# First layer of a four-layer image network: rescaled rows on GpSimd in slot 8, two of a band's four layer norm operations on VectorE

## Chip, cores and metric

The kernel runs on one core of a Trainium2 chip. The metric is the device time of one execution in microseconds (us); the lower the better. All data are float32.

## What is computed

The reference takes an image batch `x` of shape (4, 64, 64, 128) and adds four residual layers to it in turn: `x = x + layer(group_norm(x))`. Only the first layer matters here. It is a selective scan over the 4096 pixels of each image in four directions:

```python
xz = x @ in_proj_w.T                       # x is the group-normed image
xh, z = jnp.split(xz, 2, axis=-1)          # 256 channels each
z  = silu(z)
xc = silu(depthwise_conv3x3(xh) + conv_b)
xs = [xc by rows, xc by columns, both reversed]        # K = 4 directions
...                                        # delta, B, C: small projections of xs
h  = exp(delta * A) * h + (delta * u) * B  # step by step over 4096 pixels, 16 states
y  = sum(h * C) + D * xs                   # the four directions are added
y  = (y - mean) / sqrt(var + eps) * out_norm_w + out_norm_b    # layer norm of a pixel
y  = y * z
out = y @ out_proj_w.T
```

The other three layers (Fourier mixing, a Fourier neural operator with attention, neighbourhood attention) follow after it and are the same code before and after the change.

## The kernel before

**Units and slots.** The first layer walks through 128 units: 4 images, 4 directions, 8 chunks of 512 pixels. A unit has 16 slots, one for each of the 16 states, so there are 2048 slots. The numbers of slots below run from 0 to 15 in a unit. In every slot the code issues the following, in this order:

- GpSimd: `dB = du * B` (line 699, 128x1024). There are three `dB` buffers, so GpSimd can be up to three slots ahead of the scans.
- VectorE: what was put off to this slot with `later("dve", ...)`, and then the steps that `TABLE` gives it.
- ScalarE and VectorE, twice (once for each half of the channels): `dA = exp(delta * A)` into one of three PSUM banks (line 704) and the scan `h` (`tensor_tensor_scan`, line 705), which reads `dA` and `dB`.
- TensorE: eight transposes of an older slot's `h` into the single PSUM tile `pt` (line 549), and eight products `yT` with C (line 584). ScalarE copies `pt` to `hT` (line 559).
- What was put off to `act2`, which is the last place of the slot on ScalarE.
- TensorE: steps of the next unit's projections, such as `dp` (line 475), and in slots 10 and 12, after the `dB` of that slot, GpSimd's `du = delta * u` (line 487). `du` waits for VectorE's `delta` of slots 9 and 11 (line 484).

**Order.** The order on each engine is the order in which the code issues, written out by hand (`tc.manual_schedule`). `later(place, f, ..., slots=n)` puts an operation off by `n` slots.

**Side work.** Two generators are threaded through the slots, one piece at a time. A piece runs in a slot that the sets of `SIDE` allow for its kind, and when its share of the unit's slots is due.

- `before(b + 1)` prepares the next image while image b is scanned: statistics, then for each of eight chunks `c` a DMA `load` of ten padded rows (`xn`), the operation `scaled`, which applies the group norm to `xn` in place (line 326), two products for the gate z (kind `z`, slots 13 and 1), and for each half `s` a 3x3 convolution as nine TensorE pieces `t` = 0 to 8 (kind `c`, starting in slot 11 and then one in every slot up to slot 3 of the next unit; line 159). The rows of chunk `c + 1` are loaded at piece (s, t) = (0, 0) of chunk `c`, and scaled after piece (1, 5). One chunk takes three units.
- `after(b)` finishes image b while image b + 1 is scanned, in eight bands of 512 pixels. For images 0 and 1 (`b + 2 < NB`), piece `t` computes `nb = 1/sqrt(var + eps)` on ScalarE (line 388), puts off the small product `mb = -mean * nb` (a 128x4 operation on VectorE) by two slots, and puts off the four normalisations `y[:, q, :] = y * nb + mb` (128x256) on ScalarE by two, three, four and five slots. Two pieces `m` transpose the band to `pg` and ScalarE writes it to `yg`; GpSimd multiplies by z in slot 7 (line 414); the output projection follows in slot 8 (line 424).

For image 2 the normalisations are done by the existing helper `normed` on VectorE, with the factor in PSUM; image 3 has no following image. The helper, which the change also uses:

```python
nb = spare("nb")[:, 0:4]                      # images 2 and 3: PSUM
nb = small.tile([P, 4], F32, name="nb")       # images 0 and 1: SBUF
```

In the profile, operations that are issued by `flush` have the line of `later`'s list (L645) and are told apart by the names of their tiles: `mb`, `yf` (the band), `yg`, `e` (the steps of silu).

Of the kernel before, what the change touches and what calls it, by code (L numbers as in the profile page):

```python
# [12 lines left out]
AF = mybir.ActivationFunctionType  # L13
ALU = mybir.AluOpType
# [10 lines left out]
NCH = NT // CH  # L25
# [57 lines left out]
def layer0(sh, A, x_in, x_out, scr, ahead):  # L83
# [6 lines left out]
    tc, nc = sh.tc, sh.nc  # L90
    with ExitStack() as ctx:
# [60 lines left out]
        def conv(xn, s, bank, out):  # L152

            for t in range(9):
                yield "c"
                if t == 0:
                    pm = bank("cv")
                dy, dx = divmod(t, 3)
                nc.tensor.matmul(  # L159
                    pm,  # L160
                    lhsT=taps[:, s, t, :],
                    rhs=xn[:, dy : dy + 8, dx : dx + 64],
                    start=(t == 0),
                    stop=(t == 8),
                )
            out.append(pm)
# [6 lines left out]
        def gates(b, c, v, bank, later, es=(None, None)):  # L173
            for s in range(2):
                yield "z"
                zp = bank("zp")
                nc.tensor.matmul(zp, lhsT=w_in[:, 2 + s, :], rhs=v, start=True, stop=True)
                silu(zp, 0.0, 0.0, scr(f"z{b % 3}")[s, :, c * CH : (c + 1) * CH], later, (("act0", 2), ("act0", 3), 4), es[s])
# [126 lines left out]
        def before(b, bank, later):  # L305

            st = small.tile([P, NCH, 6], F32, name="gn_st")
            for c in range(NCH):  # L310
                yield "l"
                t = tmp.tile([P, CH], F32, name="xs", tag="t2", bufs=4)
                nc.sync.dma_start(t.rearrange("p (h w) -> p h w", w=64), A["x_t"][b, :, 8 * c + 1 : 8 * c + 9, 1:65])
                yield "s"
                later("dve", nc.vector.bn_stats, st[:, c, :], t)
            yield "m"
            s_, o_ = sh.group_scale(st, psm, small, "m", exp_rstd)

            def load(c):
                xn = tmp.tile([P, 10, 66], F32, name="xn", bufs=3)  # L320
                nc.sync.dma_start(xn, A["x_t"][b, :, 8 * c : 8 * c + 10, :])
                return xn

            def scaled(xn, c, r0, r1):
                inner = xn[:, max(r0, int(c == 0)) : min(r1, 10 - int(c == NCH - 1)), 1:65]
                nc.scalar.activation(inner, inner, AF.Identity, scale=s_, bias=o_)

            yield "l"
            ahead = load(0)
            yield "x"  # L330
            later("act2", scaled, ahead, 0, 0, 10)
            for c in range(NCH):
                xn = ahead
                yield from gates(b, c, xn[:, 1:9, 1:65], bank, later)
                for s in range(2):
                    for t, piece in enumerate(conv(xn, s, bank, out := [])):
                        yield piece
                        if c < NCH - 1 and (s, t) == (0, 0):
                            ahead = load(c + 1)
                        if c < NCH - 1 and s == 1 and t == 5:  # L340
                            later("act2", scaled, ahead, c + 1, 0, 10)
                    grown(b, c, s, out[0], later)

        def silu(v, bias, minus, dst, later, wait, e=None):
# [22 lines left out]
        def after(b, st, later, bands):  # L367

            for c in bands:
                yield "l"  # L370
                rows = slice(c * CH, (c + 1) * CH)
                if kept:
                    y = kept.pop()
                else:
                    y = tmp.tile([P, 4, 2 * P], F32, name="yf", tag="t4", bufs=4)
                    nc.sync.dma_start(y, tiles(scr(f"y2{b % 2}")[rows, :]))
                z = tmp.tile([P, 2, CH], F32, name="zf", tag="t4", bufs=4)
                nc.sync.dma_start(z, scr(f"z{b % 3}")[:, :, rows].rearrange("s p t -> p s t"))
                mv = small.tile([P, 4, 2], F32, name="ln_mv")
                for q in range(4):  # L380
                    nc.vector.bn_aggr(mv[:, q, :], st[:, 4 * c + q])

                rs = small.tile([P, 4], F32, name="ln_r")
                later("act1", nc.scalar.activation, rs, mv[:, :, 1], AF.Ln, bias=sh.eps5)
                if b + 2 < NB:
                    yield "t"
                    nb = small.tile([P, 4], F32, name="nb")
                    nc.scalar.activation(nb, rs, AF.Exp, scale=-0.5)
                    mb = small.tile([P, 4], F32, name="mb")
                    later("dve", nc.vector.scalar_tensor_tensor, mb, mv[:, :, 0], -1.0, nb, ALU.mult, ALU.mult, slots=2)  # L390
                    for q in range(4):
                        norm = dict(scale=nb[:, q : q + 1], bias=mb[:, q : q + 1])
                        later("act2", nc.scalar.activation, y[:, q, :], y[:, q, :], AF.Identity, slots=2 + q, **norm)
                else:
                    yield "n"

                    nb = spare("nb")[:, 0:4]
                    nc.scalar.activation(nb, rs, AF.Exp, scale=-0.5)
                    for q in range(4):
                        later("dve", normed, y[:, q, :], mv[:, q, 0:1], nb[:, q : q + 1])  # L400
                yg = tmp.tile([P, 2, CH], F32, name="yg", bufs=2)
                for s in range(2):
                    yield "m"
                    pt = spare("pg")
                    for q in range(4):
                        nc.tensor.transpose(pt[:, q * P : (q + 1) * P], y[:, q, s * P : (s + 1) * P], sh.ident)
                    norm = dict(scale=on_w[:, s : s + 1], bias=on_b[:, s : s + 1])
                    later("act0", nc.scalar.activation, yg[:, s, :], pt, AF.Identity, **norm)
                yield "f"
                xr = tmp.tile([P, 4, DM], F32, name="xr", tag="t2", bufs=4)  # L410
                nc.sync.dma_start(xr, tiles(x_in(b)[rows, :]))
                if b < NB - 1 or c > 2:
                    yield "g"
                nc.gpsimd.tensor_tensor(yg, yg, z, ALU.mult)
                if b + 2 < NB:
                    yield "o"
                    op = psy.tile([P, 2, 2 * P], F32, name=f"yT{int(not rev)}").rearrange("p r d -> p (r d)")
                else:
                    yield "m"
                    op = spare("op")  # L420
                op = op.rearrange("p (q d) -> p q d", q=4)
                for q in range(4):
                    for s in range(2):
                        nc.tensor.matmul(
                            op[:, q, :], lhsT=yg[:, s, q * P : (q + 1) * P], rhs=w_out[:, s, :], start=(s == 0), stop=(s == 1)
                        )
                later("dve", residual, b, rows, xr, op, slots=2)
# [134 lines left out]
        def products(G, q, hT):  # L562
# [68 lines left out]
            c={11},  # L631
            g={7},
            s={11, 12, 13, 14, 15, 0, 1, 2, 3},
            t={11, 12, 15, 0},
            o={8},
            f=(),
            l=(),
# [3 lines left out]
        slot = 0  # L641

        def later(place, f, *a, slots=1, **kw):

            todo.setdefault((slot + slots, place), []).append(lambda: f(*a, **kw))  # L645
# [10 lines left out]
        with tc.manual_schedule(engines=order):  # L656
# [4 lines left out]
            for i, (b, k, c) in enumerate(units):  # L661
# [25 lines left out]
                for n in range(NS):  # L687
                    slot = NS * i + n
                    g, q = divmod(n, 4)
# [39 lines left out]
                    if n == 10:  # L729
                        y = unit["y"] = tmp.tile([P, 4, 2 * P], F32, name="y", tag="t4", bufs=4)  # L730
# [15 lines left out]
                        d.step()  # L746
                    for d in sides:
                        if d.need == "t" and n in SIDE["t"] and d.due(slot) and (inside or not any(o.taps for o in sides)):
                            d.free_at = slot + 6
                            d.step()  # L750
                        if d.need == "o" and n in SIDE["o"] and d.due(slot - 8):
                            d.step()
                        if d.need == "s" and n in SIDE["s"] and d.due(slot):
                            d.step()
                        if d.need in ("f", "l") and d.due(slot):
                            if d.need == "l":
                                d.free_at = slot + 3
                            d.step()
# [1455 lines left out]
```

## Time and profile before

| | us |
|---|---|
| median of 3 runs (lowest, highest) | 7645.87 (7638.12, 7647.14) |
| the profiled execution, its own time | 7645.85 |
| span of the profile, first to last instruction | 7644.1 |
| first layer in it, roughly | from 0 to 5600 |
| ScalarE `xn` (L326), 24 operations of 864 to 944 ns | 21.9 |
| ScalarE `yf` (L645), 64 operations, mean 604 ns | 38.7 |
| VectorE `mb` (L645), 16 operations, mean 1428 ns | 22.9 |

The page of the profile gives the busy time of each engine, the chain of work that ended last and the costliest groups of instructions. DVE is VectorE, ACT is ScalarE, POOL is GpSimd, PE is TensorE and PEld its weight loads. A group's line reads: line of the code, engine, operation, names of what is written and read, shapes, count, busy time in us and mean duration of one in ns, and after the bar the engine's idle time just before these instructions and what ended it. In a timeline, a line gives the start, the length, the engine and the instruction with the number of merged neighbours, and in brackets the idle time before it.

### The profile page before, as it was taken

What the parts mean: (1) busy time and instruction counts of PE and PEld (TensorE: products, weight loads), DVE (VectorE), ACT (ScalarE), POOL (GpSimd) and SP (SyncE); (2) the same over time, 40 slices, a digit from 0 to 9 for tenths busy, and PEclk for the clock granted to TensorE, in tenths of its full rate; (3) what the DMA queues carried; (4) which work ended last, traced back from release to release, by engine and by line L of the source; (5) the groups of instructions that cost most, each with busy time, mean ns of one, the idle gap of its engine ahead of it and who ended that gap; (6) DMA issues with size and microseconds to landing.
All of it is one profiled execution on the core that took longest, in us unless ns stands there. A gap on an engine that the chain in (4) does not pass through costs nothing.

```text
span 7644.1 us, 140402 instructions
## 1 busy us (share of the span) xinstructions
PE 6293.8 (82%) x52604; PEld 3973.6 (52%) x52604; DVE 6715.7 (88%) x7999; ACT 6135.0 (80%) x9771; POOL 5691.9 (74%) x2688
## 2 busy tenths in 40 slices
PE   7888888778898877888887777787789978686889
PEld 3554444444455544445554444454467756464556
DVE  7999999999999999999999999999956655656678
ACT  7999999999999999999999999999943323324667
POOL 4999999999999999999999999999920024123233
PEclk8999999999999999999999999999999988788999
DMA  6656566546667554565756445555533241331332
GB/s 181 171 177 176 182 175 180 171 154 178 198 180 195 184 179 160 167 196 178 183 191 180 165 169 180 179 185 174 190 92 73 59 120 46 83 99 46 102 95 82
DMA packets 1328925, 1160.66 MB, mean 152 GB/s; under 512 B 718709, under 2 KB 1119697, under 8 KB 1261298
## 3 DMA queue, kind: packets, MB, share of 16 engines
q1 hardware_dynamic: 1323970, 1149.24, 50.4%
q8 instruction: 414, 6.78, 0.4%
q10 hardware_dynamic: 4272, 2.43, 0.1%
q14 instruction: 269, 2.20, 0.1%
HBM read 958.19 MB, written 189.21 MB: 150 GB/s over the span
## 4 chain that ended last, share of the span: by engine, by line
ACT 36%; PE 31%; DVE 18%; issue 8%; POOL 3%; DMA 2%; SPq 1%; ACTq 0%; DVEq 0%; POOLq 0%
ACT hT L559 14%; ACT dA L704 14%; DVE h L705 12%; PE pt L549 5%; PE cv L159 3%; POOL dB L699 3%; PE yT L584 3%; PE pf L939 2%; PE po L952 1%; ACT e L645 1%; ACT delta L478 1%; PE yT L458 1%; PE pz L1183 1%; PE pt L1892 1%; ACT delta L481 1%
## 5 line engine op out<-in xcount | busy, mean ns | idle before, releaser
L705 DVE TENSOR_TENSOR_SCAN h<-dA,state,dB 128x512 f32<-128x512 f32 x4096 | 4927.0, 1266 | 120.7 <-ACT dA L704 72.4
L699 POOL TENSOR_TENSOR dB<-du,Bb 128x1024 f32<-128x1024 f32 x2048 | 4816.5, 2387 | 152.3 <-DVE h L705 118.2
L549 PE MATMUL pt<-ident,h 128*128 128x128 f32 x16384 | 2216.7, 278 | 859.2 <-ACT hT L559 833.8
L704 ACT ACTIVATE dA<-delta,A_neg 128x512 f32<-128x512 f32 x4096 | 2765.5, 696 | 102.7 <-DVE h L705 77.0
L549 PEld LDWEIGHTS pt<-ident,h 128*128 128x128 f32 x16384 | 1802.7, 141 | 1917.7 <-ACT hT L559 1700.5
L559 ACT COPY hT<-pt 128x1024 f32<-128x1024 f32 x2048 | 2080.7, 1016 | 125.5 <-PE pt L549 105.9
L584 PE MATMUL yT<-hT,W 128*32 128x256 f32 x16384 | 1378.6, 409 | 4.3 <-DVE xr L433 3.5
L584 PEld LDWEIGHTS yT<-hT,W 128*32 128x32 f32 x16384 | 456.2, 150 | 346.3 <-issue 324.3
L159 PE MATMUL cv<-xn,taps 128*128 128x512 f32 x936 | 527.1, 645 | 2.7 <-DVE delta L484 2.6
L1183 POOL TENSOR_TENSOR xg<-xg,so 128x1024 f32<-128x1024 f32 x16 | 39.3, 2469 | 622.8 <-PE pu L1183 622.2
L1930 POOL TENSOR_TENSOR S<-S,sm 128x784 f32<-128x784 f32 x128 | 191.1, 1493 | 416.3 <-DVE sm L1928 250.0
L487 POOL TENSOR_TENSOR du<-delta,u 128x512 f32<-128x512 f32 x256 | 327.8, 1281 | 163.6 <-DVE delta L484 162.2
L475 PE MATMUL dp<-xd,w_dt 65*128 65x512 f32 x512 | 288.7, 646 | 33.8 <-DVE delta L484 23.7
L458 PE MATMUL yT<-u,w_x 128*48 128x512 f32 x508 | 244.4, 604 | 21.3 <-DVE y L600 20.1
L1937 ACT ACTIVATE S<-S,mx 128x196 f32<-128x196 f32 x512 | 227.9, 448 | 33.2 <-DVE mx L1964 32.7
L159 PEld LDWEIGHTS cv<-xn,taps 128*128 128x128 f32 x936 | 139.2, 188 | 180.5 <-issue 160.4
L940 ACT ACTIVATE h<-pf,b 128x512 f32<-128x512 f32 x128 | 87.6, 687 | 118.8 <-PE pf L939 100.5
L484 DVE SCALAR_TENSOR_TENSOR delta<-delta,dp 128x512 f32<-128x512 f32 x256 | 169.7, 663 | 3.2 <-ACT delta L481 1.0
L1183 POOL TENSOR_TENSOR WX<-wr,Xs 128x544 f32<-128x544 f32 x40 | 59.3, 1483 | 149.1 <-issue 63.4
L1892 PE MATMUL pt<-ident,S 128*98 128x128 f32 x1024 | 165.6, 286 | 3.5 <-POOL S L1930 2.0
L481 ACT ACTIVATE delta<-delta 128x512 f32<-128x512 f32 x256 | 164.5, 643 | 0.0
L478 ACT ACTIVATE delta<-dp 128x512 f32<-128x512 f32 x256 | 152.3, 595 | 10.4 <-PE dp L475 9.2
(381 smaller groups left out, 6921.7 us busy)
## 6 DMA issues: line engine op xcount, KB each, us to landing
Bb<-l_B SPq DMA_DIRECT2D x512, 1024.0 KB
W<-l_W SPq DMA_DIRECT2D x512, 256.0 KB
l_y<-y SPq DMA_DIRECT2D x127, 512.0 KB
u<-l_xr SPq DMA_DIRECT2D x64, 512.0 KB
u<-l_xw SPq DMA_DIRECT2D x64, 512.0 KB
y<-l_y SPq DMA_DIRECT2D x56, 512.0 KB
V<-l_v SPq DMA_DIRECT2D x512, 49.0 KB
y<-l_y SPq DMA_DIRECT2D x80, 256.0 KB
```

The lines of the kernel that those rows point to most:

```text
L159: nc.tensor.matmul(pm, lhsT=taps[:, s, t, :], rhs=xn[:, dy : dy + 8, dx : dx + 64], start=(t == 0), stop=(t == 8),)
L458: nc.tensor.matmul(bank["x"], lhsT=w_x[:, s, k, :], rhs=u[:, s, :], start=(s == 0), stop=(s == 1))
L475: nc.tensor.matmul(bank[s], lhsT=w_dt[:, k, s * P : (s + 1) * P], rhs=xd, start=True, stop=True)
L481: nc.scalar.activation(delta[:, s, :], delta[:, s, :], AF.Ln, bias=1.0)
L487: nc.gpsimd.tensor_tensor(du[:, s, :], delta[:, s, :], u[:, s, :], ALU.mult)
L549: nc.tensor.transpose(pt[:, j, s, :], G["h"][:, s, t0 : t0 + 32, :].rearrange("p t n -> p (t n)"), sh.ident)
L559: return lambda: nc.scalar.copy(hT, pt.rearrange("p j s d -> p j (s d)"))
L584: nc.tensor.matmul(U["yT"][e][32 * jo : 32 * jo + 32, qo % 2, :], lhsT=U["Ws"][G["g"]][:, :, 4 * q + j], rhs=hT[:, j, :], start=((e, jo) n ...
L699: nc.gpsimd.tensor_tensor(dB, du, B_now[:, q : q + 1, :].to_broadcast([P, 2, CH]), ALU.mult)
L704: nc.scalar.activation(dA, delta[:, s, :], AF.Exp, scale=A_neg[:, k, s, n : n + 1])
L705: nc.vector.tensor_tensor_scan(h[:, s, :, q], dA, dB[:, s, :], state[:, s, n : n + 1], ALU.mult, ALU.add)
L1892: nc.tensor.transpose(pt[:, half, hp, :], U["S"][:, e, hp, 98 * half : 98 * half + 98], sh.ident)
```

## The change

```diff
@@ before(): scaled
-                nc.scalar.activation(inner, inner, AF.Identity, scale=s_, bias=o_)
+                nc.gpsimd.tensor_scalar(inner, inner, s_, o_, ALU.mult, ALU.add)
@@ before(): the call of it
-                        if c < NCH - 1 and s == 1 and t == 5:
-                            later("act2", scaled, ahead, c + 1, 0, 10)
+                        if c < NCH - 1 and s == 0 and t == 8:
+                            later("act2", scaled, ahead, c + 1, 0, 10, slots=5)
@@ after(): images 0 and 1
-                    later("dve", nc.vector.scalar_tensor_tensor, mb, mv[:, :, 0], -1.0, nb, ALU.mult, ALU.mult, slots=2)
+                    later("dve", nc.vector.scalar_tensor_tensor, mb, mv[:, :, 0], -1.0, nb, ALU.mult, ALU.mult, slots=3)
                     for q in range(4):
+                        if q % 2:
+                            later("dve", normed, y[:, q, :], mv[:, q, 0:1], nb[:, q : q + 1], slots=3 + q)
+                            continue
                         norm = dict(scale=nb[:, q : q + 1], bias=mb[:, q : q + 1])
-                        later("act2", nc.scalar.activation, y[:, q, :], y[:, q, :], AF.Identity, slots=2 + q, **norm)
+                        later("act2", nc.scalar.activation, y[:, q, :], y[:, q, :], AF.Identity, slots=3 + q, **norm)
@@ SIDE
-            t={11, 12, 15, 0},
+            t={12},
@@ step of "t"
-                            d.free_at = slot + 6
+                            d.free_at = slot + 7
```

`normed` is `nc.vector.scalar_tensor_tensor(y, y, mean, factor.to_broadcast([P, 2 * P]), ALU.subtract, ALU.mult)`. The rows of a chunk are now scaled by GpSimd, in slot 8 of the unit before the one in which ScalarE scaled them (a piece that ends in slot 3, put off by five slots). The first chunk of an image is scaled where it was, also by GpSimd. With piece `t` in slot 12, `mb` comes in slot 15, the normalisations q = 0 and q = 2 on ScalarE in slots 15 and 1, and q = 1 and q = 3 on VectorE at the start of slots 0 and 2 of the next unit.

## Prediction

> **What bounds the kernel now.** I read the first section of the page, then the windows of the four images (about 113 to 1481, 2866, 4249 and 5600 us), then the timelines of one band, then the chain of waits. The windows show three engines nearly full together:
>
> ```profile
> 1481.00:2866.00 1385.00, 1167.87 (x9092) 682.99 (x9092) 1346.62 (x1269) 1324.97 (x1923) 1301.35 (x589) 1.00 0.61 181
> ```
>
> The columns are PE, PEld, VectorE, ScalarE, GpSimd, clock, DMA. VectorE is busy 97%, ScalarE 96%, GpSimd 94%. None can be named from shares; the bound must be found slot by slot. The groups by shape show what is touched:
>
> ```profile
> L645 ACT ACTIVATE yf<-yf,mb,nb 128x256 f32<-128x256 f32 x64 | 38.7, 604 | 0.8 <-DVE mb L645 0.8
> L645 DVE SCALAR_TENSOR_TENSOR mb<-ln_mv,nb 128x4 f32<-128x4 f32 x16 | 22.9, 1428 | 0.0
> L430 DVE SCALAR_TENSOR_TENSOR yf<-yf,ln_mv,nb 128x256 f32<-128x256 f32 x56 | 22.8, 468 | 0.0
> L326 ACT ACTIVATE xn<-xn,gn_o,gn_s 128x640 f32<-128x640 f32 x18 | 16.7, 927 | 0.0
> ```
>
> The nearest GpSimd operation to the new one stands in a later layer (shortest, median and longest in ns, first and last start):
>
> ```profile
> L1183 POOL TENSOR_SCALAR m<-m,scal x16: 2838/2843/3780, 6461.9 to 6997.1; 128x1024 f32<-128x1024 f32 x16
> ```
>
> `mb` has four columns and takes 1.43 us, while `normed` with 256 takes 0.47. The timelines of GpSimd and VectorE round one `mb` tell why:
>
> ```profile
> 2119.07 9.43 POOL L699 TENSOR_TENSOR dB<-du,Bb 128x1024 f32<-128x1024 f32 x4
> 2128.68 9.44 POOL L699 TENSOR_TENSOR dB<-du,Bb 128x1024 f32<-128x1024 f32 x4 [0.18 <-DVE h L705]
> ```
> ```profile
> 2124.71 1.46 DVE L645 SCALAR_TENSOR_TENSOR mb<-ln_mv,nb 128x4 f32<-128x4 f32 x1
> 2126.09 9.53 DVE L705 TENSOR_TENSOR_SCAN h<-dA,state,dB 128x512 f32<-128x512 f32 x8
> 2136.34 9.65 DVE L705 TENSOR_TENSOR_SCAN h<-dA,state,dB 128x512 f32<-128x512 f32 x8 [0.72 <-ACT dA L704]
> ```
>
> Four `dB` in 9.43 us have edges at 2119.07, 2121.43, 2123.79, 2126.14 and 2128.50. `mb` starts inside the third and ends at 2126.17, on its edge: it waited for GpSimd. All 16 `mb` end so, 1.20 to 1.99 us long. The 0.72 us idle at 2136.34 is ScalarE's fault: four `yf` and one `xn` have just passed there. So a band is first VectorE-bound (1.4 us lost to `mb`), then ScalarE-bound.
>
> A convolution slot has a third limit. The chain in slots 1 to 3 reads:
>
> ```profile
> 1736.97 0.87 PE pt L549 x8
> 1737.84 0.60 PE yT L584 x8
> 1738.44 1.06 PE cv L159 x2
> ```
>
> That is 2.53 us of TensorE in a slot, against 2.37 for two scans.
>
> **What the skill says.** The Trainium skill, SBUF — State Buffer, section Who interferes with whom: a VectorE instruction with two SBUF inputs contends with a GpSimd instruction that reads SBUF, and whichever issues second blocks until the first is done. The `mb` edges agree. `normed` for image 2 (0.449 to 0.477 us) never blocks, and its factor lies in PSUM; in the change `nb` is in SBUF, so q = 1 and q = 3 fall under the rule. The GPSIMD Engine Reference, section Engine selection, calls one-input operations roughly line-rate. The trace differs: `m` takes 2.84 us for 1024 columns, more than the two-input `dB` with 2.39.
>
> **Part 1, rows on GpSimd.** Removed from ScalarE: 24 operations, 21.9 us. Added to GpSimd: 24. No row shows this form (two steps, 10 rows of 64). Lower end 1.78 us, `m` scaled by 640/1024; upper end 3.6 us, twice that for two steps. I take 1.9 us. Cover: before `du` in slot 10, GpSimd idles, for scans and then for `delta`. In image 0:
>
> ```profile
> 691.49 2.38 POOL L699 TENSOR_TENSOR dB<-du,Bb 128x1024 f32<-128x1024 f32 x1 [0.27 <-DVE h L705]
> 694.49 2.39 POOL L699 TENSOR_TENSOR dB<-du,Bb 128x1024 f32<-128x1024 f32 x1 [0.62 <-DVE h L705]
> 697.95 1.28 POOL L487 TENSOR_TENSOR du<-delta,u 128x512 f32<-128x512 f32 x1 [1.07 <-DVE delta L484]
> ```
>
> 0.27 + 0.62 + 1.07 = 1.96 us, and in image 1 (2105.18 to 2111.91) 0.28 + 0.63 + 1.34 = 2.25. The operation lies behind the `dB` of slot 8 and before this idle time, so 1.9 us cost nothing. Queued behind it are the later `dB` and `du`. Above 1.96 us they slip; by slot 13 GpSimd is only some 0.3 us ahead of the scans (end of `dB` against start of its scan in the timelines), so VectorE waits from 2.3 us on. The loads and SP's queue are unmoved; rows loaded 13 slots (34 us) earlier have landed. Three first chunks stay in slot 0 or 1, where GpSimd is 2.1 to 2.8 us ahead: nothing.
>
> The gain where ScalarE loses `xn`: scans start at 715.31 and 728.38 (slots 0 and 5, with `xn`), 13.07 us; the unit before, with a convolution and no `xn`, takes 673.01 to 685.93, 12.92. TensorE's 2.53 a slot replaces ScalarE. So 0.15 us, not 0.92: seven in image 0, 1.0 us; two lone ones in images 1 and 2, 0.3.
>
> **Part 2, the bands.** ScalarE loses 32 of 64 `yf`, 19.3 us. VectorE gains 32 of 0.47, 15.0 us, plus blocking. The edits of `SIDE["t"]` and `free_at` move nothing: all 16 `mb` already stood in slot 14, so `t` was in slot 12, and the band's transposes come eight slots after the new release (`yg` at 2162.57, slot 12). Worked through the band at 2124.71:
>
> - Slot 14 without `mb`: `dA` is ready at 2124.78, the scan starts at 2124.85 and slot 15 is reached at 2127.15. GpSimd is inside the `dB` that ends at 2128.50. `mb` waits 1.35 us and the scan starts at 2128.46; before, it was 2128.47. Moving it gains nothing.
> - q = 1: two scans later, at 2130.75, the next `dB` ends at 2130.86. Wait 0.11, own 0.47. Scan 2131.28, before 2130.81. GpSimd's next `dB` needs the scan that has just ended, so it can't slip in first.
> - q = 3: VectorE arrives at 2135.95; a `dB` that started 0.2 us after a scan ended runs to 2136.2. Wait 0.25, own 0.47. Scan of slot 2 at 2136.62, before 2136.34: 0.28 late, because the 0.72 us idle is filled.
> - Behind these on VectorE wait the scans, and for them GpSimd's `dB` and ScalarE's three `dA` banks. In slot 4 ScalarE made VectorE wait 0.1 us before; that goes, so VectorE is 0.17 late at slot 5.
> - ScalarE: without two `yf` and `xn` it is bounded by TensorE's convolution, and the `e` of slot 4 needs its end; as in image 0 it gains some 0.2 us. VectorE's next idle time (0.87 + 0.31 at 2167.75, behind `xw` and two `yg`) hides the 0.17 and passes on the 0.2.
>
> So about 0.2 us gained in 12 bands that have an `xn` beside them: 2.4. Two bands (2648, 4033) run into units where VectorE has no idle time for 18 us: 1.2 lost each; two (1691, 3075) have 0.86 idle in slot 6 and lose 0.3 each: together 3.0.
>
> **Sum.** Minus 1.0, 0.3 and 2.4, plus 3.0: minus 0.7 us. The profiled execution took 7645.85, the median 7645.87, so no correction: 7645.
>
> **Rivals.**
> 1. *ScalarE's relief counts.* For: the chain of the page gives ScalarE 36%, VectorE 18%. If TensorE catches up within the slots, each of 12 bands gains the whole 1.18 us idle of slot 14, 14 us, and nine lone `xn` 0.8 each, 7: 7625. Against: the twin stretches of image 0. Chance 0.2.
> 2. *Collisions, slower.* `normed` arrives just after a `dB` has begun, in slots 0 and 2, and waits 2.4 us each time. It decides once blocking exceeds the 1.2 us of idle time that follows. At half a `dB` each, 16 x 1.2 = 19 us: 7665; at a whole one, 58 us: 7703. For: `mb` waits 1.43 us on average. Against: `mb` itself sets VectorE on a `dB` edge just ahead. Chance 0.13.
> 3. *GpSimd's operation is dear.* At 3.6 us it overruns by 1.3 in image 0 (some 0.3 hidden by ScalarE's `xw`), 7 us, and delays the edge that `mb` waits for by up to 1.2 in 12 bands, 14: 7666. From 2.3 us on it costs anything. Chance 0.09.
> 4. *Nothing contends* (an input broadcast from four columns might not count): 0.36 us less in 16 bands, 6 us, inside the main case.
>
> **Numbers.** 0.2% is 15 us, about what a measurement of this kernel tells from no change. The main case, within 0.2%, has 0.58; its own range is 7631 to 7661. Faster by more is 0.2 (rival 1), slower 0.22 (rivals 2 and 3). The range reaches to their nearer ends: 7624 to 7668.
>
> **What would show it.** In the profile after: `xn` on GpSimd near 1.9 us and `du`'s wait for `delta` shorter by about that in every third unit; `mb` in slot 15, still some 1.4 us, ending on a `dB` edge; the new `yf` on VectorE between 0.47 and 0.75 us; VectorE's idle time in slot 2 nearly gone, and in slot 14 still there. I am wrong if `xn` takes over 2.3 us and VectorE waits for `dB` in slot 13, if `yf` on VectorE averages over 1.5 us, or if the idle time in slot 14 vanishes.

## The result and the profile after

| | before | after |
|---|---|---|
| median, us (lowest to highest; 17 runs each) | 7644.61 (7638.12 to 7651.99) | 7632.98 (7626.97 to 7635.81) |
| ratio, 95% interval | | 0.9983 [0.9977, 0.9989] |
| span of the profiled execution, us | 7644.1 | 7625.9 |
| last pair of scans of the first layer starts, us | 5591.80 | 5581.29 |

The kernel became 11.6 us faster by the medians, and 0.17% by the ratio. The interval leaves no doubt about the sign. The median lies inside the predicted range (7624 to 7668), but 12 us below the predicted value of 7645: a gain of 0.7 us was predicted from the kernel before, and 11.6 us were measured. The spans of the two profiled executions differ by more, 18.2 us. Only 10.5 us of that lie in the first layer; the rest falls in layers whose code is the same, so it is a difference between two executions. I therefore use the start of the last pair of scans in the first layer as the mark for all profiles below. The timelines of VectorE before and after, with the start and the length first:

```profile
5591.80 2.46 DVE L705 TENSOR_TENSOR_SCAN h<-dA,state,dB 128x512 f32<-128x512 f32 x2 [2.16 <-POOL dB L699]
```
```profile
5581.29 2.46 DVE L708 TENSOR_TENSOR_SCAN h<-dA,state,dB 128x512 f32<-128x512 f32 x2 [2.15 <-POOL dB L702]
```

Lines in the kernel after stand three lower than in the kernel before (`dB` L702, the scan L708, `normed` L433, `later`'s list L648). The groups by shape of after, cut to the touched operations in the first layer:

```profile
L433 DVE SCALAR_TENSOR_TENSOR yf<-yf,ln_mv,nb 128x256 f32<-128x256 f32 x88 | 38.8, 480 | 0.0
L648 DVE SCALAR_TENSOR_TENSOR mb<-ln_mv,nb 128x4 f32<-128x4 f32 x16 | 20.8, 1298 | 0.0
L648 ACT ACTIVATE yf<-yf,mb,nb 128x256 f32<-128x256 f32 x32 | 19.2, 601 | 2.3 <-DVE mb L648 2.2
L326 POOL TENSOR_SCALAR xn<-xn,gn_s,gn_o 128x640 f32<-128x640 f32 x18 | 16.1, 895 | 0.0
```

`xn` takes 0.90 us on GpSimd, half of the 1.9 us that the prediction took and below its lower end of 1.78. The new `yf` on VectorE barely wait: the 88 of the line average 480 ns, against 468 for the 56 of before, and the 32 new ones alone 498. `mb` still waits, 1.30 us on average against 1.43 (1.14 without one of 3.64 us, which comes up below). The window of image 1 shows that the work has moved, and that no engine has been relieved of much (columns PE, PEld, VectorE, ScalarE, GpSimd, the clock granted to TensorE as a share of its full speed, DMA):

```profile
1481.00:2866.00 1385.00, 1167.91 (x9118) 684.63 (x9119) 1355.72 (x1288) 1316.02 (x1904) 1313.52 (x599) 1.00 0.61 181
```

VectorE is up by 9 us, GpSimd by 12, and ScalarE is down by 9. The band that the prediction worked through looks like this on VectorE after the change:

```profile
2125.62 1.27 DVE L648 SCALAR_TENSOR_TENSOR mb<-ln_mv,nb 128x4 f32<-128x4 f32 x1
2126.82 2.45 DVE L708 TENSOR_TENSOR_SCAN h<-dA,state,dB 128x512 f32<-128x512 f32 x2
2129.18 0.45 DVE L433 SCALAR_TENSOR_TENSOR yf<-yf,ln_mv,nb 128x256 f32<-128x256 f32 x1
2129.56 4.80 DVE L708 TENSOR_TENSOR_SCAN h<-dA,state,dB 128x512 f32<-128x512 f32 x4
2134.28 0.55 DVE L433 SCALAR_TENSOR_TENSOR yf<-yf,ln_mv,nb 128x256 f32<-128x256 f32 x1
2134.75 9.51 DVE L708 TENSOR_TENSOR_SCAN h<-dA,state,dB 128x512 f32<-128x512 f32 x8
...
2165.39 1.28 DVE L708 TENSOR_TENSOR_SCAN h<-dA,state,dB 128x512 f32<-128x512 f32 x1 [0.47 <-ACT dA L707]
```

`mb` still takes 1.27 us to write four columns. q = 1 takes 0.45 us and q = 3 takes 0.55. The idle time of 0.72 us in slot 2 is gone, as predicted. The one in slot 14 of the next unit was predicted to stay, and about half of it went: 0.47 us are left where it was 0.87, and the five scans before it take 5.98 us where they took 6.19. ScalarE's timelines show who waits in slot 2, before and after:

```profile
2135.53 1.31 ACT L704 ACTIVATE dA<-delta,A_neg 128x512 f32<-128x512 f32 x2
```
```profile
2136.05 0.70 ACT L707 ACTIVATE dA<-delta,A_neg 128x512 f32<-128x512 f32 x1 [0.33 <-DVE h L708]
```

Before, the scan of 2136.34 waited for the `dA` that starts at 2135.53. After, ScalarE is ahead: its second `dA` waits for a scan to free a bank. Measured from the scan of slot 12 of the band's unit, the scan of slot 2 comes at 16.33 us (16.32 before), while its `dA` comes at 14.48 (15.52 before). GpSimd's timeline shows where the rows went:

```profile
2103.34 0.87 POOL L326 TENSOR_SCALAR xn<-xn,gn_s,gn_o 128x640 f32<-128x640 f32 x1
2104.18 4.80 POOL L702 TENSOR_TENSOR dB<-du,Bb 128x1024 f32<-128x1024 f32 x2
2110.32 1.28 POOL L490 TENSOR_TENSOR du<-delta,u 128x512 f32<-128x512 f32 x1 [1.33 <-DVE delta L487]
```

The operation stands in front of two `dB`, which now follow each other without the 0.28 and 0.63 us of idle time of before; and GpSimd still idles 1.33 us for `delta` before `du` (1.34 before, where a shorter wait was predicted). So the rows delay nothing that GpSimd does here.

**Slot by slot.** Subtracting the scan starts of two profiles slot by slot gives the place of each gain. By the end of images 0, 1 and 2 the change stands at −1.5, −5.4 and −10.3 us. Single units jump by up to 1 us either way, with no edit near them. The larger of these jumps lie where the record of TensorE's granted clock shows 0.50 for 3.4 or 6.8 us. Unit 66, for example, has such a stretch of 3.4 us before and one of 6.8 us after, and is 1.08 us longer after. The windows of 6.8 us, before and after, have a mean clock (the last number but two) of 0.75 and 0.50:

```profile
2987.30:2994.10 6.80, 6.13 (x47) 3.74 (x45) 5.92 (x6) 6.35 (x11) 4.96 (x3) 0.75 0.76 284
```
```profile
2980.40:2987.20 6.80, 6.16 (x32) 4.51 (x36) 4.40 (x7) 4.02 (x8) 4.56 (x3) 0.50 0.82 335
```

In e2, where no row is moved, unit 66 is longer by the same 1.08 us, and in e5 and e6, where the stretch has 3.4 us again, by 0.05 and −0.03. Unit 60 is 0.8 us shorter in every profile than in the one before, which alone has a stretch of 6.8 us across the start of that unit. So the sums are good to some 2 us.

### The profile page after: what moved, and what is told of

Its sections match the earlier page's. It is cut to its first block, busy times and chain, and to the rows that moved or that the text cites. A ratio compares the mean times of both kernels' runs of the same rounds, so it can differ in the third digit from the quotient of the medians.

```text
span 7625.9 us, 140413 instructions
## 1 busy us (share of the span) xinstructions
PE 6282.4 (82%) x52604; PEld 3970.3 (52%) x52604; DVE 6725.7 (88%) x8031; ACT 6102.3 (80%) x9715; POOL 5712.2 (75%) x2712
## 4 chain that ended last, share of the span: by engine, by line
ACT 33%; PE 33%; DVE 20%; issue 8%; POOL 3%; DMA 2%; SPq 1%; ACTq 0%; DVEq 0%; POOLq 0%
ACT hT L562 13%; DVE h L708 13%; ACT dA L707 12%; PE pt L552 6%; PE cv L159 4%; PE yT L587 3%; POOL dB L702 3%; PE pz L1186 2%; PE pf L942 2%; ACT e L648 1%; PE po L955 1%; ACT delta L481 1%; PE yT L461 1%; PE pt L1895 1%; ACT delta L484 1%
## 5 line engine op out<-in xcount | busy, mean ns | idle before, releaser
L708 DVE TENSOR_TENSOR_SCAN h<-dA,state,dB 128x512 f32<-128x512 f32 x4096 | 4927.9, 1266 | 99.7 <-ACT dA L707 53.1
L702 POOL TENSOR_TENSOR dB<-du,Bb 128x1024 f32<-128x1024 f32 x2048 | 4820.4, 2393 | 118.8 <-DVE h L708 90.2
L1186 DVE TENSOR_TENSOR WX<-wr,Xs 128x544 f32<-128x544 f32 x88 | 75.8, 877 | 97.4 <-PE pz L1186 69.0
```

The costliest lines, as they stand in the source:

```text
L702: nc.gpsimd.tensor_tensor(dB, du, B_now[:, q : q + 1, :].to_broadcast([P, 2, CH]), ALU.mult)
L708: nc.vector.tensor_tensor_scan(h[:, s, :, q], dA, dB[:, s, :], state[:, s, n : n + 1], ALU.mult, ALU.add)
L1186: r = f(*args, **kw)
```

## Experiments

Theory A is the prediction's picture with a smaller price of `xn`: part of the gain is the rows', part the bands'. Its rival B says that the rows alone carry it. Each kernel was timed beside the kernel before, whose median was 7645.6 us beside e1 to e4 and 7645.7 us beside e5 to e8. The last column is from one profile each.

| | median, us | ratio [95%] | last scans of the first layer, us |
|---|---|---|---|
| e1 rows alone | 7630.11 | 0.998 [0.9973, 0.9988] | 5577.38 |
| e2 bands alone | 7645.20 | 0.9999 [0.9991, 1.0008] | 5594.93 |
| e3 the change, `mb` in columns | 7632.91 | 0.9983 [0.9977, 0.999] | 5582.36 |
| e4 all `yf` on GpSimd | 7631.16 | 0.9981 [0.9973, 0.999] | 5579.85 |
| e5 rows, `mb` in columns | 7630.68 | 0.998 [0.9971, 0.9989] | 5576.36 |
| e6 all `yf` on GpSimd, other form | 7628.26 | 0.9979 [0.9972, 0.9986] | 5574.02 |
| e7 rows, still in slot 1 | 7629.58 | 0.9979 [0.9971, 0.9986] | 5580.21 |
| e8 rows, dearer operation | 7644.31 | 0.9998 [0.999, 1.0006] | 5592.50 |

**e1, the rows alone.** The kernel before with only the first two hunks of the change:

```diff
-                nc.scalar.activation(inner, inner, AF.Identity, scale=s_, bias=o_)
+                nc.gpsimd.tensor_scalar(inner, inner, s_, o_, ALU.mult, ALU.add)
-                        if c < NCH - 1 and s == 1 and t == 5:
-                            later("act2", scaled, ahead, c + 1, 0, 10)
+                        if c < NCH - 1 and s == 0 and t == 8:
+                            later("act2", scaled, ahead, c + 1, 0, 10, slots=5)
```

> Only the rows go to GpSimd (slot 8); the bands stay as they were, four normalisations on ScalarE and mb in slot 14. The whole change gained 11.6 us in the median, and the scans of the first layer ended about 10.5 us earlier in the profile. Theory A (each part alone meets the next limit: without xn, TensorE's 2.53 us of a convolution slot, since four yf slots of 2.63 leave it no slack): about 0.15 us for each of 21 chunks and some 1.5 for the three first chunks, so 4 to 5 us in all, and VectorE's idle time in slot 14 of the unit after a band (behind xw and two yg) stays at 1.2 us. Rival B (the gain is the rows' alone: VectorE's 0.7 to 0.9 us of waiting behind xn was the whole price): 0.7 x 12 bands plus 1.5 in image 0 and 1.5 for first chunks, 10 to 12 us, the same as the whole change.

The gain is 15.5 us, at least that of the whole change, and the profile's first layer is 14.4 us shorter. Rival B holds. The timeline of VectorE round the same band:

```profile
2119.30 1.43 DVE L645 SCALAR_TENSOR_TENSOR mb<-ln_mv,nb 128x4 f32<-128x4 f32 x1
2120.66 19.07 DVE L705 TENSOR_TENSOR_SCAN h<-dA,state,dB 128x512 f32<-128x512 f32 x16
...
2161.48 1.28 DVE L705 TENSOR_TENSOR_SCAN h<-dA,state,dB 128x512 f32<-128x512 f32 x1 [0.88 <-ACT dA L704]
```

Sixteen scans follow `mb` without a pause, where before the eighth was followed by 0.72 us of idle time. And the idle time in slot 14 is as long as before (0.88 against 0.87 us), so what was won in slot 1 was not given back there. In 12 band units the scans gain some 0.8 us in slot 1 (0.82 in the one shown) and keep nearly all of it: 9.6 us in sum. A chunk of image 0, which has no band beside it, gains 0.81 in slot 1 and gives back 0.15, 0.16 and 0.35 in slots 2 to 4. The first chunks of the three images bring another 3.3 us, in units 5, 35 and 67. With 0.8 us of image 0 and 0.3 of the two lone chunks this makes 14.0 of the 14.4 us.

**e2, the bands alone.** The change with `xn` back on ScalarE, in its old slot.

```diff
-                nc.gpsimd.tensor_scalar(inner, inner, s_, o_, ALU.mult, ALU.add)
+                nc.scalar.activation(inner, inner, AF.Identity, scale=s_, bias=o_)
-                        if c < NCH - 1 and s == 0 and t == 8:
-                            later("act2", scaled, ahead, c + 1, 0, 10, slots=5)
+                        if c < NCH - 1 and s == 1 and t == 5:
+                            later("act2", scaled, ahead, c + 1, 0, 10)
```

> Only the bands change (mb in slot 15, q = 1 and q = 3 on VectorE in slots 0 and 2); the rows stay on ScalarE in slot 1. Theory A: VectorE's added 1.3 us in a band fills only part of a wait that stays (xn still holds ScalarE up in slot 1), so between 0 and 4 us gained, and the two parts together are worth more than their sum. Rival B (rows alone): no change or a loss of some us. Rival C (the bands are the whole gain): 8 us or more. The new yf on VectorE stay at 0.45 and 0.54 us in all.

No change that a measurement tells. In image 1 six bands with an `xn` beside them gain 0.2 to 0.3 us each (they lose 0.4 in slot 15 to q = 1, and gain 0.35 to 0.6 in slot 1; three of them 0.1 in slot 4), and the two bands in units without idle time lose some 0.7 us each in slots 15 to 4. The profile's first layer ends 3.1 us later than before, of which 2.7 us arise in slots 7 and 8 of unit 105, long after the last band that was edited, where the granted clock is 0.50 for 6.8 us. Rows and bands together are not worth more than the rows alone.

**e3, `mb` without a wait.** `mb` is computed a column at a time, by an operation whose only tensor input is one column of `mv`:

```diff
-                    later("dve", nc.vector.scalar_tensor_tensor, mb, mv[:, :, 0], -1.0, nb, ALU.mult, ALU.mult, slots=3)
+                    for q in (0, 2):
+                        later("dve", nc.vector.tensor_scalar, mb[:, q : q + 1], mv[:, q, 0:1], nb[:, q : q + 1], -1.0, ALU.mult, ALU.mult, slots=3)
```

> The changed kernel with mb computed as two one-column operations with two pointer scalars (only columns 0 and 2 are used), so that it has one SBUF tensor input and should not wait for GpSimd. Theory A1 (mb's wait, mean some 1.2 us, is lost time of VectorE, which is the bound there): mb takes about 0.2 us in two operations and a band gains up to 0.7 us, 16 bands up to 11 us. Rival (mb's wait is what sets VectorE on an edge of dB, so that the two normed operations after it find the port free): the new yf on VectorE lose their 0.45 and 0.54 us and wait 1 us or more each, and the kernel is no faster or slower than the change by some us.

The time is that of the change. VectorE's timeline shows why:

```profile
2126.17 0.31 DVE L649 TENSOR_SCALAR mb<-ln_mv,nb 128x1 f32<-128x1 f32 x2
2126.40 2.45 DVE L709 TENSOR_TENSOR_SCAN h<-dA,state,dB 128x512 f32<-128x512 f32 x2
2128.76 1.27 DVE L434 SCALAR_TENSOR_TENSOR yf<-yf,ln_mv,nb 128x256 f32<-128x256 f32 x1
```

Two `mb` now take 0.31 us. But `mb`'s wait had set VectorE on the edge of a `dB`; without it the next operation with two inputs, `yf` of q = 1, waits in its place. The group of `yf` rose from 480 to 632 ns (88 operations, so 13 us of waiting came back, all of it in the 32 new ones), and one took 4.17 us. So `yf` on VectorE does collide with `dB`; in the change `mb`'s wait just before it keeps it clear.

**e4, all `yf` on GpSimd.** Instead of `mb`, ScalarE and VectorE, four operations `(y − mean) * nb` on GpSimd, in slots 7 and 8 of the next unit (the release of the band moves with them).

```diff
+        def rows_normed(y, mean, factor):
+            nc.gpsimd.tensor_scalar(y, y, mean, factor, ALU.subtract, ALU.mult)
...
+                        later("act2", rows_normed, y[:, q, :], mv[:, q, 0:1], nb[:, q : q + 1], slots=11 + q // 2)
```

> The changed kernel with all four normalisations of a band on GpSimd as (y - mean) * nb, two in slot 7 and two in slot 8 of the unit after (11 and 12 slots after t), no mb, nothing of it on VectorE or ScalarE. GpSimd took 0.9 us for 640 columns, so 0.4 us for 256: 1.6 us in a band, and it idles 0.6 + 1.7 us there before du in slots 9 and 10. Theory A: VectorE loses 1.2 us of waiting and 1.0 us of own work in each of 16 bands and ScalarE 1.2; what is bounded by TensorE's 2.53 us and by xw and two yg stays, so 8 to 20 us faster than the change. Rival (GpSimd is as full as it looks, 94 to 95%): du and dB slip and VectorE waits for dB in slot 13, no faster than the change.

No faster than the change by a measurement, as the rival had it. The tile's own line (shortest, median and longest in ns) gives 1.23 us for 256 columns, and then VectorE waits for GpSimd:

```profile
L427 POOL TENSOR_SCALAR yf<-yf,ln_mv,nb x64: 1211/1229/1292, 1711.1 to 4044.9; 128x256 f32<-128x256 f32 x64
```
```profile
2157.93 4.81 DVE L705 TENSOR_TENSOR_SCAN h<-dA,state,dB 128x512 f32<-128x512 f32 x4 [0.42 <-POOL dB L699]
...
2163.86 7.20 DVE L705 TENSOR_TENSOR_SCAN h<-dA,state,dB 128x512 f32<-128x512 f32 x6 [1.12 <-POOL dB L699]
```

In the band of before, the scan after the second `delta` waited for nothing and the next for ScalarE. Over image 1 the idle time of VectorE before its scans that a `dB` ended rose from 3.7 to 13.5 us, while that which `dA` ended fell from 25.0 to 10.9. Four operations at 1.23 us exhaust GpSimd's lead: in the 12 band units 0.5 to 0.9 us are lost in slots 7 to 11. But as much comes back in slots 12 to 15, and over three units these bands gain 1.0 us each, no less than in e6 below and more than the 0.84 of e1. In slots 2 to 6 they give back 0.66 us, as in e6, where TensorE is the limit. The first layer of the profile ends 2.5 us after that of e1 all the same; 1.6 us of this lie ahead of the first scan, and 1.1 in unit 34, where e4's clock is at 0.50 for 6.8 us and e1's for 3.4. So GpSimd's waits are shown, but not that they are what keeps e4 at e1's time.

**e5, is `mb`'s wait worth anything?** e1 with `mb` as four one-column operations on VectorE. Nothing is moved beside it, so no `yf` of image 0 or 1 can inherit the wait.

```diff
-                    later("dve", nc.vector.scalar_tensor_tensor, mb, mv[:, :, 0], -1.0, nb, ALU.mult, ALU.mult, slots=2)
+                    for q in range(4):
+                        later("dve", nc.vector.tensor_scalar, mb[:, q : q + 1], mv[:, q, 0:1], nb[:, q : q + 1], -1.0, ALU.mult, ALU.mult, slots=2)
```

> The kernel with only the rows on GpSimd, and mb (in slot 14) as four one-column operations with pointer scalars, 0.2 us each, in place of one of 1.43 us that waits for GpSimd. Theory A2 (in a band ScalarE is the limit from xw in slot 13 to the end of silu in slot 5, with four yf slots of 2.63 us, and mb's wait lies in its shadow; in that kernel's profile VectorE is back at ScalarE's heels, 0.1 us behind, at slot 5): mb shrinks by some 0.7 us and the kernel stays within 3 us of the rows alone. Rival (VectorE is the limit there and mb's wait is lost time): 0.7 x 16, some 11 us faster than the rows alone.

The same time as e1 (7630.68 against 7630.11 us). The wait went, and VectorE now waits for ScalarE instead, as its timeline shows:

```profile
2119.87 0.55 DVE L646 TENSOR_SCALAR mb<-ln_mv,nb 128x1 f32<-128x1 f32 x4
2120.34 4.88 DVE L706 TENSOR_TENSOR_SCAN h<-dA,state,dB 128x512 f32<-128x512 f32 x4
2125.37 2.47 DVE L706 TENSOR_TENSOR_SCAN h<-dA,state,dB 128x512 f32<-128x512 f32 x2 [0.16 <-issue]
2128.02 2.46 DVE L706 TENSOR_TENSOR_SCAN h<-dA,state,dB 128x512 f32<-128x512 f32 x2 [0.18 <-ACT dA L705]
```

In e1 `mb`'s 1.4 us and the four `yf` of ScalarE ran beside each other; taking away one leaves the other.

**e6, the form of the operation.** e4 with `y * nb + mb` (multiply, add), one in each of slots 4 to 7, and `mb` by column on GpSimd.

```diff
+        def minus(out, mean, factor):
+            nc.gpsimd.tensor_scalar(out, mean, factor, -1.0, ALU.mult, ALU.mult)
+        def rows_normed(y, factor, offset):
+            nc.gpsimd.tensor_scalar(y, y, factor, offset, ALU.mult, ALU.add)
...
+                        later("act2", minus, mb[:, q : q + 1], mv[:, q, 0:1], nb[:, q : q + 1], slots=7)
+                        later("act2", rows_normed, y[:, q, :], nb[:, q : q + 1], mb[:, q : q + 1], slots=8 + q)
```

> All four normalisations of a band on GpSimd, as in the kernel before this one, but in the form y * nb + mb (multiply, add) that the rows have, with mb as four one-column operations on GpSimd, and one normalisation in each of slots 4 to 7. There (y - mean) * nb took 1.23 us for 256 columns, the rows' form 0.88 us for 640. If the form decides, a normalisation takes 0.35 to 0.45 us, VectorE no longer waits for dB in slots 11 and 13 of the unit after the band, and the kernel is 3 to 10 us faster than the rows alone (in a band, TensorE's 2.53 us in a slot is then the limit: about 0.4 us in 16 bands beyond the rows). If the shape decides (one row of 256 against ten of 64), it stays at 1.2 us and the kernel is no better than with all four in the subtracting form.

```profile
L432 POOL TENSOR_SCALAR yf<-yf,nb,mb x64: 538/573/622, 1702.0 to 4036.5; 128x256 f32<-128x256 f32 x64
```

The same 256 columns now cost 0.57 us instead of 1.23. The first layer of the profile ends another 3.4 us earlier than in e1, and the median of 7628.26 is the lowest of all versions, though a measurement does not tell it from e1. Here the chain of waits tells what the limit is. The same stretch in e1, and then in e6 (start, length, what):

```profile
2125.25 1.01 ACT hT L559
2126.26 0.50 ACT yf L645
2126.76 0.77 ACT dA L704 x2
2127.53 0.36 issue
2127.89 1.01 ACT hT L559
```
```profile
2125.64 0.87 PE pt L554 x8
2126.52 0.60 PE yT L589 x8
2127.12 1.06 PE cv L159 x2
2128.18 0.87 PE pt L554 x8
```

In e1 a slot with a `yf` takes ScalarE 2.63 us (`hT` to `hT`, 2125.25 to 2127.89), and no convolution stands in the chain. In e6 ScalarE has no `yf`, the chain is TensorE's and the slot takes 2.53. In its band units the loss in slots 2 to 4 that was known from image 0 appears again: −0.88, then +0.16, +0.17 and +0.34.

**e7, the rows in their old slot.** One line of the kernel before is changed: `scaled` runs on GpSimd, in slot 1 as before.

> The kernel before with one line changed: the rows scaled by GpSimd, but where ScalarE scaled them, in slot 1. Theory A: at 0.9 us GpSimd, which is 0.6 to 2.2 us ahead of the scans in slot 1, hides it there too, so the gain is that of the rows in slot 8, 12 to 16 us, and the place is worth nothing. Rival (slot 8 is what hides it, before du's wait): GpSimd slips, VectorE waits for dB, half of the gain or less.

7629.58 us, against 7630.11 for e1. At 0.9 us the slot makes no difference that a measurement tells. (The profile ends 2.8 us after that of e1: 1.4 us lie ahead of the first scan, and 1.1 in unit 34, where e7's clock is at 0.50 for 6.8 us and e1's for 3.4.)

**e8, a dearer operation in the same place.** e1 with another pair of operations, `(x - o) * s` instead of `x * s + o`; only its time is of interest, since its values are not those of the group norm:

```diff
-                nc.gpsimd.tensor_scalar(inner, inner, s_, o_, ALU.mult, ALU.add)
+                nc.gpsimd.tensor_scalar(inner, inner, o_, s_, ALU.subtract, ALU.mult)
```

> The rows alone in slot 8, in the dear form (x - o) * s in place of x * s + o, which leaves the group norm's offset wrong: only the price of the operation is of interest. By 1.23 us for 256 columns it takes some 3 us for 640. Theory (idle time of GpSimd of 2.0 to 2.25 us before du covers it, and 0.3 us of lead by slot 13): it overruns by 0.5 to 0.8 us, VectorE waits for dB in slots 11 to 13 of every third unit, and of the rows' gain of some 15 us 5 to 12 are given back. Rival (it is free whatever it costs, or the form is no dearer here): as fast as the rows alone.

The operation took 2.5 us and the whole gain was gone (7644.31 us). In the views by tile of `xn` and `mb`:

```profile
L326 POOL TENSOR_SCALAR xn<-xn,gn_o,gn_s x24: 2282/2505/2564, 332.1 to 3879.2; 128x640 f32<-128x640 f32 x18, 128x576 f32<-128x576 f32 x6
```
```profile
L645 DVE SCALAR_TENSOR_TENSOR mb<-ln_mv,nb x16: 1205/1446/3958, 1689.5 to 4031.3; 128x4 f32<-128x4 f32 x16
```

Four of the 16 `mb` took 3.9 us, 2.5 us more than the usual wait, which accounts for 9.9 of the 15 us by which the first layer ended later than in e1. Another 2.5 us arise in units 47 and 76, just behind two of these waits. TensorE had been idle for some 2 us there, and then its granted clock was 0.50 for 3.4 us. The rest lies in other jumps of single units and ahead of the first scan.

Everywhere else the dear operation cost nothing: the chunks of image 0 gain the same 0.15 us as in e1, and over image 1 VectorE idled 3.0 us for `dB` before its scans, against 4.1 in e1. So the overrun of 0.5 to 0.8 us in every third unit, which was expected, did not come. The prediction's third rival had said that it costs from 2.3 us on. It did cost at 2.5, but neither by the waits for `dB` that the rival names nor by an edge that is 1.2 us later in 12 bands: the other 12 `mb` wait as long as in e1. That the threshold seems to fit is luck.

## Why the prediction was right, and which term was off

The measured 7632.98 us lies even in the main case's own range (7631 to 7661). But that range is 0.2% to both sides of a sum that foresaw a gain of 0.7 us, so the hit is its width's more than the sum's. The change did what the first rival describes, at a smaller size.

**Right.** *The waits of VectorE.* `mb` moved one slot and gained nothing: 1.27 us in the band shown, and all 16 still end within 0.03 us of an edge of `dB`. For q = 1 and q = 3 it had waits of 0.11 and 0.25 us on top of 0.47; they took 0.45 and 0.55. So the second rival (collisions of `yf`, 7665 to 7703) is refuted for this order of slots, and e3 shows that it was close: shift VectorE off the edge, and the collisions come. The rule of the Trainium skill on which both rest (SBUF — State Buffer, section Who interferes with whom: of two such instructions the second blocks until the first is done) is borne out by e3, since a one-column `mb` without a second tensor input took 0.20 us and did not wait, while `yf` in the next slot waited 0.8 us. That the block can last longer than one instruction is shown below.

*The chunks without a band.* The step "So 0.15 us, not 0.92" gave 1.0 us for seven in image 0; measured are 0.9 (unit 21, between them, gave 0.14 back), and 0.15 and 0.14 for the two lone ones. *The rows delay nothing on GpSimd*, and the slot did not matter (e7).

*Bands that meet no idle time.* 1.2 us each was expected at 2648 and 4033. Against the kernel before, the scans lose 1.1 and 0.7 us there (a jump of 0.64 in the first, which e1 and e2 show as well, left out; 0.4 of its 1.1 us lie at a stretch with the clock at 0.50). The two at 1691 and 3075, for which 0.3 each was expected, came out at 0.0 and +0.1.

**Wrong in size.** *The price of `xn`*: 1.9 us taken, 0.9 measured, below the lower end. The row of `m` was the wrong twin, since it multiplies only and yet costs 2.84 us for 1024 columns. The error cost nothing, as both prices fit under the cover of 1.96 us; and e8 shows that in image 0 even 2.5 us cost nothing, so the cover was reckoned too small. What a price of 2.5 us set off were the double waits of `mb`.

*The term that decided* is "as in image 0 it gains some 0.2 us" and its sum, "So about 0.2 us gained in 12 bands", 2.4 us. The 12 bands gained 0.72 to 0.95 us each, save one, and 11 of them come to 9.4 us. I had carried the twin stretches of image 0, where TensorE's 2.53 us per slot takes over, to units in which it does so only in part. The time from one `hT` of ScalarE to the next, from slot 1 to slot 2 and from slot 2 to slot 3, shows it. In image 0 (unit 17) 2.96 and 2.24 us became 2.53 and 2.53: a gain of 0.43, of which 0.29 go back at once. Beside the band shown, 3.44 and 2.27 became 2.63 and 2.25 in e1: a gain of 0.81, and nothing goes back, since the slots with a `yf` are bound by ScalarE at 2.63 us, and TensorE, at 2.53, does not hold it up. In the change they became 2.63 and 2.56: again 0.81, of which 0.29 go back.

So the path of the prediction was right for the change: the relief reaches VectorE at its idle time in slot 14. The size was not. In the band shown `dA` comes 0.83 us earlier than before at slot 5 and 0.75 at slot 14, not 0.2; the scans are 0.11 us early at slot 5 (0.17 late was predicted), stay so up to slot 11, and gain 0.6 in slots 12 and 13. Over the 12 bands slots 12 and 13 bring 0.15 to 0.62 us, and in e2, where `xn` stays on ScalarE, no more than 0.12. This is the first rival, with 0.86 us per band where it had 1.18. In e1, where q = 1 and q = 3 don't fill VectorE's idle time, the same relief is cashed in slot 1 at once, and VectorE runs 16 scans without a pause. In e6, with no `yf` on ScalarE, TensorE's limit is back in slots 2 to 4.

The gain is moreover the rows' alone. With `xn` gone, the bands' edit adds less than 0.1 us per band (0.86 us on average over those 11 bands, against 0.80 in e1), though alone it brings 0.2 to 0.3 (e2): both edits take from the same idle time. For the three parts of the change this means: the rows bring 15 us; `mb` in slot 15 and `yf` on VectorE bring nothing on top, and in the profiles the first layer of the change ends 3.9 us after that of e1 (10.5 us gained against 14.4). Of these 2.4 are one event; the intervals of the two ratios overlap, so a cost in the time itself is not shown. The event stands in the timelines of VectorE and of GpSimd after:

```profile
1994.48 3.64 DVE L648 SCALAR_TENSOR_TENSOR mb<-ln_mv,nb 128x4 f32<-128x4 f32 x1
```
```profile
1986.36 11.74 POOL L702 TENSOR_TENSOR dB<-du,Bb 128x1024 f32<-128x1024 f32 x5
2000.64 2.47 POOL L702 TENSOR_TENSOR dB<-du,Bb 128x1024 f32<-128x1024 f32 x1 [2.53 <-DVE h L708]
```

This `mb` waited to the end of the fourth `dB` (near 1995.7), did not get its turn, and waited through the fifth to 1998.1. That band lost 1.6 us where its neighbours won 0.8 to 0.9. The prediction had no such case.

*Left out*: the first chunks of the images. I had given them nothing, since only GpSimd's lead was looked at; ScalarE's relief counts there too: −0.57 us in unit 5, and −1.2 and −1.4 in the first slots of units 35 and 67, together 3.1 us. These shifts are in every profile with the rows on GpSimd, within some 0.15 us, and in e2 they are 0.0.

The sum by these terms: −0.9 −0.3 −3.1 −9.4, plus 1.6 for the band with the double wait and 1.9 for the four other bands, is −10.2 us, and −10.5 is measured. The jumps of units 34 and 66 (+0.4 and +1.1) and of units 59 and 60 (−1.4) nearly cancel.

## What to carry to other kernels

A twin stretch tells what an engine's relief is worth only where the same engine is next. Before carrying 0.15 us from one stage to another, write down the slot time of each engine in that other stage (here 2.63 on ScalarE, 2.53 on TensorE, 2.37 on VectorE). Try the parts of a change alone: here one line (e7) gave all of the gain, and the rest of the change moved work between two full engines and added nothing. And a wait that is taken away in an order of this kind goes to the next instruction that can wait; ask which one that is, as e3 and e5 did.

## What the runs showed of the hardware

- **The pair of operations sets the price on GpSimd.** `tensor_scalar` with multiply and add took 0.90 us for 640 columns and 0.57 for 256; with subtract and multiply 2.5 and 1.23. From each two values, an estimate of 0.84 and 3.3 ns per column on top of 0.36 and 0.38 us (the 640 columns are ten rows of 64, the 256 are one row). The Trainium skill (GPSIMD Engine Reference, section Engine selection) calls operations with one input roughly line-rate. The first form agrees in that it is as fast as ScalarE, which took 0.93 us for the same rows; the second does not.
- **A blocked VectorE instruction does not always get the next turn.** In most cases it starts at the edge of the `dB` that blocks it, but 1 of 16 `mb` in the kernel after (3.64 us), 4 of 16 in e8 (3.9 us) and one `yf` in e3 (4.17 us) waited through a second one. None did in the kernel before, nor in e1, e2 and e7. What decides was not found.
- **Such a wait can cost twice.** In all six TensorE was then idle for 1.8 to 2.3 us. After three of them (units 47 and 76 of e8, unit 37 of e3) its granted clock was 0.50 for 3.4 us, and the next unit took 1.2 to 1.3 us longer than without; after the other three it stayed at 1.00.
